# Feed-forward products of a graph layer, in groups of two row blocks instead of four

## The chip, the cores and the metric

The kernel runs on one core of one Trainium2 chip. The metric is the device time of one execution in microseconds (us). Before the change it was 6551.81 us, the median of three runs (6546.44 to 6563.14). One further execution was recorded by the hardware profiler; its span is 7257.0 us, and every duration below that comes from the profile belongs to that execution.

## The reference

Two layers of a graph network over 10,000 nodes of 512 features and 160,000 edges, all in fp32. Cut to what matters:

```python
# layer 0
h   = relu(layernorm(x))
msg = einsum('nd,rdf->nrf', h, rel_W)[src, edge_type]       # 4 relations
agg = segment_sum(msg, dst) / max(deg, 1)
x1  = layer_norm(h + h @ self_W + agg) * ln1_w + ln1_b
f   = gelu(x1 @ W1 + b1) @ W2 + b2                          # 512 -> 1024 -> 512
x   = x + layer_norm(x1 + f)
# layer 1
h   = relu(layernorm(x))
for W_self, W_neigh, b in both:                             # twice
    h = relu(h @ W_self + (segment_sum(h[src], dst) / max(deg, 1)) @ W_neigh + b)
x   = x + h
```

## The kernel before

Nodes are worked in 79 blocks of 128 rows; the last one, block 78, has 16 rows and is worked first. The program has four stages, one behind the other.

**First stage.** For every block the four relation products of `h` are computed and written to `hall_d` in HBM; beside that, the edge list is turned into lists of row numbers.

**The feed-forward stage** is the one that the change edits. For every block it gathers the message rows of the block from `hall_d`, sums them, normalises, does the two feed-forward products, normalises twice more, and writes `h1_d` and `xn_d`. The third and the fourth stage do the same gathers, from `h1_d` and then from `h2_d`, with two products of 512 x 512 per block.

**Gathers.** `gather` (L655 to L671) issues them on GpSimd's queue (POOL), each an indirect DMA of 128 rows of 2 KB: five `orow` tiles (called others), then eleven `row` tiles (called mine), and before them a `tail` tile every fourth and every sixteenth block. That makes 1276 gathers in each of the three gather stages. All but the tails go through one ring of `RING = 28` buffers (L648), which serves the three stages; a gather can be issued when the tile 28 places before it has been read. Others and tails are summed by seven fp32 products with 0/1 matrices on TensorE (`sums`, L688), mine by eleven adds on VectorE into the same PSUM tile (`add`, L700). In the profile an fp32 product is two MATMUL rows, each with its own weight load.

**Slots.** The order is written out by hand (manual schedule): engines run their instructions in program order. The loop over blocks makes one slot per block. In a slot for block b, VectorE first adds the second residual of blocks that were fed forward one slot ago (`second`, L851), then adds the mine rows of b and computes the statistics of b; TensorE does the part of the feed-forward work that stands next in `queue`; ScalarE computes the square roots of the statistics (`now.finish`, L829) and the normalised rows (`scaled`, L837), issued ahead of the last item of that part; the slot ends with the gathers and the sum products of block b+1 (`begin`).

**Groups.** `Group` holds four blocks (128 x 512 moving columns). `turn` (L772, L774) transposes the normalised block on TensorE into one of two PSUM tiles and scales it into `x1T` on ScalarE; it stands in the middle of the slot after the block's own. `up` (L784, L786) makes one of eight 128-column parts of `x1 @ W1` for all four blocks, eight MATMUL rows of 512 columns into one of two PSUM banks, and applies Gelu. `down` (L795) makes a block's product with `W2`, sixteen rows of 512 columns, and issues the load of the residual `xr` on SyncE's queue. `parts` cuts a group into four slots: four `up`, four `up`, two `down`, two `down`. They are queued behind the first slot of the next group.

**The end of the stage.** After the last block, the loop `while queue or fed or third` works off what is queued: half of the ups and all downs of the last group of four, and the ups and downs of a last pair. The row numbers are then shifted by two bits on VectorE (L953), since the later tables have one row per node, and the third stage begins. Its gathers read `h1_d`, so that the first one waits until the last write of `h1_d` (L867) has landed.

Of the kernel before, what the change touches and what calls it, by code (L numbers as in the profile page):

```python
# [16 lines left out]
P = 128  # L17
# [4 lines left out]
def kernel(  # L22
# [621 lines left out]
    def aligned(ctxa):  # L644

        gat = ctxa.enter_context(tc.tile_pool(name="gat", bufs=1))
        psA = ctxa.enter_context(tc.tile_pool(name="psA", bufs=2, space=PSUM))
        RING = 28  # L648
        rest = list(range(full))
        blocks = ([full] if N % P else []) + rest  # L650

# [51 lines left out]
        with ExitStack() as s:  # L703
            wp = s.enter_context(tc.tile_pool(name="wp2", bufs=1))
            gp = s.enter_context(tc.tile_pool(name="gp", bufs=1))
            sp = s.enter_context(tc.tile_pool(name="sp", bufs=3))
            psT = s.enter_context(tc.tile_pool(name="psT2", bufs=2, space=PSUM))
            psH = s.enter_context(tc.tile_pool(name="psH", bufs=2, space=PSUM))
            psO = s.enter_context(tc.tile_pool(name="psO", bufs=2, space=PSUM))
            w1s = wp.tile([P, KC, F], F32, name="w1s")  # L710
            w2s = wp.tile([P, FC, D], F32, name="w2s")
# [5 lines left out]
            def pair(t, b, n, name, bufs):  # L717

                return (gp.tile([P, 2, D], F32, name=name, bufs=bufs)[:height(b), :n],
                        rows_of(t, (b, n, height(b))))  # L720
# [10 lines left out]
            def load_res(b, n):  # L731
                v, at = pair(xr_d, b, n, "xr", 3)
                nc.sync.dma_start(v, at)
                for c in range(n):
                    xrs[b + c] = v[:, c, :]
                xrs[b, n] = v
# [22 lines left out]
            class Group:  # L759


                def __init__(self, bs):
                    self.bs, self.r = bs, height(bs[0])
                    self.xT = gp.tile([P, KC, 4 * P], F32, name="x1T", bufs=2)
                    self.hid = None

                def turn(self, b, v):
# [7 lines left out]
                                             AF.Identity, bias=ln1bc[:, k:k + 1],  # L775
                                             scale=ln1wc[:, k:k + 1])

                def up(self, f):
                    n = len(self.bs) * self.r
                    if self.hid is None:  # L780
                        self.hid = gp.tile([P, FC, 4 * P], F32, name="hid")
                    ph = psH.tile([P, 4 * P], F32, name="ph")
                    for k in range(KC):
                        nc.tensor.matmul(ph[:, :n], w1s[:, k, f * P:(f + 1) * P],  # L784
                                         self.xT[:, k, :n], start=(k == 0), stop=(k == KC - 1))
                    nc.scalar.activation(self.hid[:, f, :n], ph[:, :n], AF.Gelu,  # L786
                                         bias=b1s[:, f:f + 1], scale=1.0)

                def down(self, b):
                    c, r = self.bs.index(b), self.r  # L790
                    if c % 2 == 0:
                        load_res(b, min(2, len(self.bs) - c))
                    po = psO.tile([P, D], F32, name="po")
                    for f in range(FC):
                        nc.tensor.matmul(po[:r], self.hid[:, f, c * r:(c + 1) * r], w2s[:, f, :],  # L795
                                         start=(f == 0), stop=(f == FC - 1))
                    return b, po

                def parts(self):

                    ups = [lambda f=f: self.up(f) for f in range(FC)]
                    downs = [lambda b=b: self.down(b) for b in self.bs]
                    return [ups[:FC // 2], ups[FC // 2:]] + [downs[i:i + 2]
                                                             for i in range(0, len(downs), 2)]

            COLS = 8

# [32 lines left out]
            rests = {}  # L840
            fed, third = [], []
            now = Scales()

            def second():

                nonlocal fed
                got = []
                for b, po in fed:
                    r = height(b)
                    v = rests.pop(b)  # L850
                    nc.vector.tensor_tensor(v[:r], po[:r], v[:r], op=OP.add)  # L851
                    got.append((b, v, now.stats(v[:r], r)))
                fed = []
                return got

            def scaled(got, first):

                nonlocal third, now
                if first:
                    b, c = first  # L860
                    r, v = height(b), nodes[b]
                    now.apply(v[:r], v[:r], c, r, AF.Identity)
                if third:
                    h1, at = pair(h1_d, third[0][0], len(third), "h1", 2)
                    for k, (b, c) in enumerate(third):
                        now.apply(h1[:, k, :], xrs.pop(b), c, height(b), AF.Relu)
                    nc.sync.dma_start(at, h1)  # L867
                third = []
                for b, v, c in got:
                    r = height(b)  # L870
                    now.apply(v[:r], v[:r], c, r, AF.Identity)
                if first:
                    b, c = first
                    r, v = height(b), nodes[b]
                    rests[b] = gp.tile([P, D], F32, name="rest", bufs=11)
                    nc.vector.tensor_tensor(rests[b][:r], v[:r], ln1w[:r], op=OP.mult)
                    nc.vector.tensor_tensor(rests[b][:r], rests[b][:r], lnb2[:r], op=OP.add)
                now = Scales()
                for b, v, c in got:
                    r = height(b)  # L880
                    nc.vector.tensor_tensor(v[:r], v[:r], ln2w[:r], op=OP.mult)
                    nc.vector.tensor_tensor(xrs[b], xrs[b], v[:r], op=OP.add)
                    third.append((b, now.stats(xrs[b], r)))
                if got:
                    b, n = got[0][0], len(got)
                    nc.sync.dma_start(rows_of(xn_d, (b, n, height(b))), xrs.pop((b, n)))

            plan = [[b] for b in blocks[:len(blocks) - len(rest)]]
            plan += [rest[:-2][i:i + 4] for i in range(0, len(rest) - 2, 4)] + [rest[-2:]]
            queue = []  # L890
            turning = None
            held = begin(blocks[0], hots(blocks[0]), table)

            def products(work, turned):


                nonlocal fed
                got = []
                for i, call in enumerate(work):
                    if i == len(work) - 1:  # L900
                        yield
                    if i == len(work) // 2 and turned:
                        turned()
                    got.append(call())
                if not work:
                    yield
                    if turned:
                        turned()
                fed = [g for g in got if g]

            i = 0
            grp = None
            for bs in plan:
                for b in bs:
                    r = height(b)
                    if b == bs[0]:
                        before, grp = grp, Group(bs)
                    if i + 2 < len(blocks):
                        load(blocks[i + 2])
                    if i + 1 < len(blocks):  # L920
                        hot = hots(blocks[i + 1])
                    got = second()
                    pa, mine = held
                    add(b, pa, mine)
                    v = nodes[b]
                    nc.vector.scalar_tensor_tensor(v[:r], pa[:r], rdeg[:r, b:b + 1], v[:r],
                                                   op0=OP.mult, op1=OP.add)
                    first = (b, now.stats(v[:r], r))
                    part = products(queue.pop(0) if queue else [], turning)
                    next(part)  # L930
                    now.finish()
                    scaled(got, first)
                    next(part, None)
                    if i + 1 < len(blocks):
                        held = begin(blocks[i + 1], hot, table)

                    if b == bs[0] and before:
                        queue += before.parts()
                    turning = lambda g=grp, b=b, v=v: g.turn(b, v)
                    i += 1  # L940
            turning()
            queue += grp.parts()
            while queue or fed or third:
                got = second()
                part = products(queue.pop(0) if queue else [], None)
                next(part)
                now.finish()
                scaled(got, None)
                next(part, None)


        for t in (row, orow, *srow):
            nc.vector.tensor_scalar(t, t, R.bit_length() - 1, None, op0=OP.logical_shift_right)  # L953
        quads = [[full]] + [rest[i:i + 4] for i in range(0, full, 4)]
        place = {b: (q, c) for q, bs in enumerate(quads) for c, b in enumerate(bs)}
        for step, (h_d, ws, wn, bs) in enumerate(((h1_d, ws1, wn1, bs1), (h2_d, ws2, wn2, bs2))):
# [388 lines left out]
```

## Time and profile before

| stretch | from, us | to, us | length, us |
|---|---|---|---|
| first stage, to the first gather of rows | 0 | 1514.47 | 1514.47 |
| gathers of the feed-forward stage | 1514.47 | 3417.5 | 1903.03 |
| no gather: the queue is worked off | 3417.5 | 3537.08 | 119.58 |
| gathers of the third stage | 3537.08 | 5359.3 | 1822.22 |
| no gather | 5359.3 | 5394.85 | 35.55 |
| gathers of the fourth stage | 5394.85 | 7225.03 | 1830.18 |
| end | 7225.03 | 7257.0 | 31.97 |

The stretches are read from the start and length of the indirect DMA instructions on POOL in the timeline. Over the whole span TensorE's matmuls (PE) are busy for 78 percent, POOL for 52, VectorE (DVE) for 50 and ScalarE (ACT) for 14. Busy shares do not say which engine bounds a stage; for that one looks at what an engine needs for one block if it never waits, and at what its waits end with. A busy time of PE counts the pipeline of a matmul, so that the spacing of matmuls has to be taken from starts, not from the mean durations.

### The profile page before, as it was taken

The numbers are of one execution on the slowest core, as the hardware profiler recorded it, in microseconds if no ns is written. First come the engines' busy times: TensorE is split into PE (matmuls) and PEld (weight loads), VectorE is DVE, ScalarE is ACT, GpSimd is POOL, SyncE is SP. The second block draws the span as 40 slices with busy tenths as digits, with TensorE's granted clock in tenths as the row PEclk, the third lists the DMA queues.
The fourth block names the chain that finished last, engine by engine and source line by source line (L and its number), as shares of the span: only waits on it lengthen the run. The fifth ranks groups of instructions, "written<-read, shape, count | busy, mean of one in ns | idle before, by whom it ended". The sixth has DMA issues, their size and how long they took to land.

```text
span 7257.0 us, 49943 instructions
## 1 busy us (share of the span) xinstructions
PE 5628.8 (78%) x14251; PEld 2540.8 (35%) x14251; DVE 3650.8 (50%) x7301; ACT 1019.6 (14%) x1667; POOL 3807.2 (52%) x3927
## 2 busy tenths in 40 slices
PE   8999999967888899888676666666666666666666
PEld 4444444423333334333333323332322232333232
DVE  6467786235666666666334333443434444444444
ACT  1000000012222333322210010101000000000000
POOL 0001110046666666665366666666656666666665
PEclk9999999988999999999888888888887888888888
DMA  4223232256777777775466667666666777776775
GB/s 168 93 105 112 95 117 88 84 178 191 215 222 223 224 231 221 213 216 182 154 206 207 204 203 210 205 205 205 205 206 209 218 210 213 221 218 213 218 223 169
DMA packets 457021, 1360.83 MB, mean 188 GB/s; under 512 B 71902, under 2 KB 71902, under 8 KB 446606
## 3 DMA queue, kind: packets, MB, share of 16 engines
q0 software_dynamic: 308768, 1008.91, 47.1%
q1 hardware_dynamic: 136174, 265.65, 10.3%
q10 hardware_dynamic: 11792, 82.97, 2.8%
q8 instruction: 114, 1.87, 0.1%
q14 instruction: 173, 1.42, 0.1%
HBM read 1150.25 MB, written 207.01 MB: 187 GB/s over the span
## 4 chain that ended last, share of the span: by engine, by line
PE 35%; issue 23%; another core or an unknown queue 17%; DVE 4%; ACT 3%; POOL 2%; DMA 1%; ACTq 0%; POOLq 0%; DVEq 0%; SPq 0%
PE pa L688 10%; PE ph L784 6%; PE pm L621 5%; PE po L795 5%; PE po L992 4%; PE po L1026 3%; DVE pa L700 2%; POOL rows L661 2%; PE pT L167 1%; ACT hTb L168 1%; ACT mTb L168 1%; ACT mb L1022 0%; DMA rows<-hall_d,row 0%; DMA rows<-h_d,row 0%
## 5 line engine op out<-in xcount | busy, mean ns | idle before, releaser
L700 DVE TENSOR_TENSOR pa<-pa,rows 128x512 f32<-128x512 f32 x2574 | 1798.5, 699 | 991.1 <-issue 676.5
L661 POOL DMA_INDIRECT rows<-h_d,row x1716 | 1668.4, 972 | 917.5 <-issue 422.8
L661 POOL DMA_INDIRECT rows<-hall_d,row x858 | 854.2, 996 | 516.7 <-issue 193.0
L688 PE MATMUL pa<-rows,hot 128*128 128x512 f32 (+1 forms) x2358 | 1082.1, 606 | 40.0 <-issue 28.0
L992 PE MATMUL po<-wns,mTb 128*128 128x512 f32 (+1 forms) x1264 | 687.2, 694 | 537.8 <-ACT mTb L168 274.5
L1026 PE MATMUL po<-wss,hTb 128*128 128x512 f32 (+1 forms) x1264 | 710.8, 715 | 507.3 <-ACT hTb L168 393.0
L621 PE MATMUL pm<-wrel,hT 128*128 128x512 f32 (+1 forms) x2528 | 1097.8, 592 | 0.0
L661 POOL DMA_INDIRECT rows<-h_d,orow x786 | 754.7, 960 | 404.3 <-issue 223.9
L784 PE MATMUL ph<-x1T,w1s 128*128 128x512 f32 (+2 forms) x1344 | 588.0, 591 | 163.0 <-issue 88.9
L621 PEld LDWEIGHTS pm<-wrel,hT 128*128 128x128 f32 (+1 forms) x2528 | 477.3, 189 | 607.6 <-issue 584.6
L688 PEld LDWEIGHTS pa<-rows,hot 128*128 128x128 f32 (+1 forms) x2358 | 454.3, 193 | 636.5 <-issue 607.8
L661 POOL DMA_INDIRECT rows<-hall_d,orow x393 | 373.2, 950 | 453.3 <-SPq L1341 327.3
L992 PEld LDWEIGHTS po<-wns,mTb 128*128 128x128 f32 (+1 forms) x1264 | 275.6, 224 | 934.5 <-issue 631.3
L795 PE MATMUL po<-w2s,hid 128*128 128x512 f32 (+1 forms) x1264 | 564.2, 598 | 33.5 <-issue 28.7
L1026 PEld LDWEIGHTS po<-wss,hTb 128*128 128x128 f32 (+1 forms) x1264 | 277.4, 231 | 888.6 <-ACT hTb L168 448.9
L688 PE MATMUL pa<-tail,hot 128*128 128x512 f32 x936 | 465.6, 615 | 69.5 <-issue 60.7
L998 DVE TENSOR_TENSOR po<-po,bss 128x512 f32<-128x512 f32 (+1 forms) x79 | 55.0, 696 | 815.9 <-remote 740.7
L494 POOL DMA_INDIRECT win<-rec_d,at x79 | 80.4, 1018 | 661.9 <-issue 568.9
L784 PEld LDWEIGHTS ph<-x1T,w1s 128*128 128x128 f32 x1344 | 258.7, 200 | 461.7 <-issue 375.1
L624 DVE TENSOR_TENSOR ha<-pm,brel 128x512 f32<-128x512 f32 (+1 forms) x316 | 217.0, 687 | 389.5 <-PE pm L621 388.9
L1002 DVE TENSOR_TENSOR ob<-po,bss 128x512 f32<-128x512 f32 (+1 forms) x79 | 54.5, 690 | 608.8 <-remote 283.1
L795 PEld LDWEIGHTS po<-w2s,hid 128*128 128x128 f32 (+1 forms) x1264 | 237.1, 190 | 318.9 <-issue 310.8
(237 smaller groups left out, 4144.6 us busy)
## 6 DMA issues: line engine op xcount, KB each, us to landing
hall_d<-ha ACTq DMA_DIRECT2D x78, 1024.0 KB
hb<-h_d SPq DMA_DIRECT2D x38, 1024.0 KB
rows<-h_d,row POOLq DMA_INDIRECT x1716
xs<-xs_d SPq DMA_DIRECT2D x39, 512.0 KB
xr<-xr_d SPq DMA_DIRECT2D x39, 512.0 KB
xn_d<-xr SPq DMA_DIRECT2D x39, 512.0 KB
h_d<-h SPq DMA_DIRECT2D x39, 512.0 KB
xg<-in_x_dram SPq DMA_DIRECT2D x19, 1024.0 KB
```

Source lines behind the costliest of these rows:

```text
L167: nc.tensor.transpose(p[:, k, :r], rows[:, k * P:(k + 1) * P], ident[:r, :r])
L168: nc.scalar.copy(dest, p[:, :, :r])
L494: nc.gpsimd.indirect_dma_start(out=win[:, c, :], out_offset=None, in_=rec_d, in_offset=bass.IndirectOffsetOnAxis(ap=at[:, c:c + 1], axis=0))
L621: nc.tensor.matmul(pm[:r], hT[:, k, :r], w[:, k, :], start=(k == 0), stop=(k == KC - 1))
L624: nc.vector.tensor_tensor(ha[:r, j - 1, :], pm[:r], brel[:r, (j - 1) * D:j * D], op=OP.add)
L661: nc.gpsimd.indirect_dma_start(out=t[:n], out_offset=None, in_=table, in_offset=bass.IndirectOffsetOnAxis(ap=idx, axis=0))
L688: nc.tensor.matmul(pa[:r], hot[:, t, :r], others[t], start=(t == order[0]), stop=(t == order[-1]))
L700: nc.vector.tensor_tensor(pa[:r], pa[:r], t[:r], op=OP.add)
L784: nc.tensor.matmul(ph[:, :n], w1s[:, k, f * P:(f + 1) * P], self.xT[:, k, :n], start=(k == 0), stop=(k == KC - 1))
L795: nc.tensor.matmul(po[:r], self.hid[:, f, c * r:(c + 1) * r], w2s[:, f, :], start=(f == 0), stop=(f == FC - 1))
L992: nc.tensor.matmul(po[:r], mT[:, k, :r], wns[:, k, :], start=False, stop=(k == KC - 1))
L1026: nc.tensor.matmul(po[:r], hT[:, k, :r], wss[:, k, :], start=(k == 0), stop=False)
```

## The change

- Groups have two blocks instead of four. `x1T` and `hid` have half the width, and `hid` has two buffers instead of one. An `up` makes two of the eight parts (2 x 8 MATMUL rows of 256 columns) into the two halves of one PSUM bank, then applies Gelu to each half. PSUM: three banks for `up` instead of two, one for `turn` instead of two.
- `parts` gives work items with a weight (four `up` of 1, two `down` of 2), and `products(left)` takes items until a weight of `left` is queued. In the slot behind a pair's second block, that block's `turn` now comes first, then both `down` of the pair before; in the next slot all four `up` of the pair, with the next block's `turn` in the middle.
- At the end the queue is worked off in steps that leave 8, 4, 2 and 0. The shift of the row numbers moves into this loop, behind the last `down`.
- `RING` is 32 instead of 28, `rest` has 8 buffers instead of 11.
- `h1`, `xn` and `xr` are written and loaded by pairs, as before.

```diff
-        RING = 28
+        RING = 32
...
-            psT = s.enter_context(tc.tile_pool(name="psT2", bufs=2, space=PSUM))
-            psH = s.enter_context(tc.tile_pool(name="psH", bufs=2, space=PSUM))
+            psT = s.enter_context(tc.tile_pool(name="psT2", bufs=1, space=PSUM))
+            psH = s.enter_context(tc.tile_pool(name="psH", bufs=3, space=PSUM))
...
-                self.xT = gp.tile([P, KC, 4 * P], F32, name="x1T", bufs=2)
+                self.xT = gp.tile([P, KC, 2 * P], F32, name="x1T", bufs=2)
...
-                ph = psH.tile([P, 4 * P], F32, name="ph")
-                for k in range(KC):
-                    nc.tensor.matmul(ph[:, :n], w1s[:, k, f * P:(f + 1) * P],
-                                     self.xT[:, k, :n], start=(k == 0), stop=(k == KC - 1))
-                nc.scalar.activation(self.hid[:, f, :n], ph[:, :n], AF.Gelu,
-                                     bias=b1s[:, f:f + 1], scale=1.0)
+                ph = psH.tile([P, 2, 2 * P], F32, name="ph")
+                for f in (f0, f0 + 1):
+                    for k in range(KC):
+                        nc.tensor.matmul(ph[:, f - f0, :n], w1s[:, k, f * P:(f + 1) * P],
+                                         self.xT[:, k, :n], start=(k == 0),
+                                         stop=(k == KC - 1))
+                for f in (f0, f0 + 1):
+                    nc.scalar.activation(self.hid[:, f, :n], ph[:, f - f0, :n], AF.Gelu,
+                                         bias=b1s[:, f:f + 1], scale=1.0)
...
-                return [ups[:FC // 2], ups[FC // 2:]] + [downs[i:i + 2]
-                                                         for i in range(0, len(downs), 2)]
+                return ([(1, lambda f=f: self.up(f)) for f in range(0, FC, 2)] +
+                        [(2, lambda b=b: self.down(b)) for b in self.bs])
...
+            def products(left, turned=None):
+                work = []
+                while sum(n for n, _ in queue) > left:
+                    work.append(queue.pop(0)[1])
+                if turned:
+                    work.insert(len(work) // 2, turned)
+                for call in work[:-1]:
+                    call()
+                yield
+                for call in work[-1:]:
+                    call()
...
-                    part = products(queue.pop(0) if queue else [], turning)
+                    if whole:
+                        turning()
+                        queue += whole.parts()
+                    part = products(8 if whole else 4, None if whole else turning)
...
+            shares = [8, 4, 2]
             while queue or fed or third:
                 got = second()
-                part = products(queue.pop(0) if queue else [], None)
+                left = shares.pop(0) if shares else 0
+                part = products(left)
                 next(part)
                 now.finish()
                 scaled(got, None)
                 next(part, None)
+                if not left:
+                    shift_rows()
```

## The prediction, made before the changed kernel ran

> **What bounds the kernel now.** I read the 40 slices first, then the busy time by stretch, then the timelines of POOL and PE, last the waits. The slices show that no single engine is full behind the first stage:
>
> ```profile
> PE   8999999967888899888676666666666666666666
> POOL 0001110046666666665366666666656666666665
> DMA  4223232256777777775466667666666777776775
> ```
>
> PE is near its limit in slices 0 to 7 (the first stage, untouched) and again nearly so in the feed-forward stage; POOL stands at six tenths in all three gather stages alike. Cut at the first and the last gather of each stage, the columns being stretch, us, then PE, PEld, DVE, ACT and POOL busy with counts, clock, DMA share and GB/s:
>
> ```profile
> 1514.47:3417.50 1903.03, 1596.05 (x3765) 703.65 (x3766) 1179.23 (x1954) 536.31 (x862) 1252.00 (x1276) 0.90 0.71 218
> 3537.08:5359.30 1822.22, 1225.12 (x2936) 547.88 (x2936) 709.94 (x989) 177.96 (x307) 1227.58 (x1276) 0.83 0.69 206
> 5394.85:7225.03 1830.18, 1204.85 (x2935) 541.32 (x2936) 764.75 (x1070) 135.36 (x232) 1242.82 (x1276) 0.82 0.71 217
> ```
>
> The stages differ widely in PE, DVE and ACT and hardly in length. What they share is 1276 gathers. POOL's timeline shows why: one gather follows another at a fixed step, 0.95 us of work and 0.30 us of gap, whatever the rest does.
>
> ```profile
> 2326.79 0.94 POOL L661 DMA_INDIRECT rows<-hall_d,orow  x1 [0.30 <-issue]
> 2328.04 0.95 POOL L661 DMA_INDIRECT rows<-hall_d,orow  x1 [0.30 <-issue]
> 2329.29 0.95 POOL L661 DMA_INDIRECT rows<-hall_d,orow  x1 [0.30 <-issue]
> ...
> 2346.16 0.95 POOL L661 DMA_INDIRECT rows<-hall_d,row  x1 [5.71 <-PE pa L688]
> ```
>
> The step is 1.253 us, so 1276 take 1599 us; a full block has 16.32 gathers, 20.45 us. The rest of each stretch is almost all long stops like the last line: the steps of 2.3 us and more exceed 1.253 by 262, 226 and 198 us in the three stretches, 686 in all (summed from the starts on POOL). PE, where it isn't stopped, needs 20.18 us for a slot (start of one L784 part to the next):
>
> ```profile
> 2273.92 7.03 PE L784 MATMUL ph<-x1T,w1s 128*128 128x512 f32 x16
> 2280.78 0.60 PE L772 MATMUL pT<-ident,xs 128*128 128x128 f32 x4
> 2281.22 7.03 PE L784 MATMUL ph<-x1T,w1s 128*128 128x512 f32 x16
> 2288.09 1.88 PE L688 MATMUL pa<-tail,hot 128*128 128x512 f32 x4
> 2289.81 4.46 PE L688 MATMUL pa<-rows,hot 128*128 128x512 f32 x10
> 2294.10 7.09 PE L784 MATMUL ph<-x1T,w1s 128*128 128x512 f32 x16
> ```
>
> So in the feed-forward stage POOL (20.45) is just ahead of PE (20.18).
>
> **Profile and timed runs.** The profiled span is 7257.0 us, the timed median 6551.8, 705 less. That is close to the 686 us of long stops: POOL's steps alone give 1514.5 + 3 x 1599 + 119.6 + 35.6 + 32.0 = 6499, 53 below the median. I conclude (it isn't shown) that the timed runs hardly have these stops and run at the gathers' pace. In the profile the waiters of a stop see a finished product late: `x1T` at 2345.46 waited for transposes of 2321.20. So I value the removal of stops at the 53 us left, not at 686.
>
> **What the Trainium skill says.** "TensorE: Matmul & The Clock Gate", section "Back-to-back issue gap", has N / 2.4 + 2.5 ns for a warm matmul of N columns, and says that in a stream of weight loads and matmuls both set the spacing. The trace has two passes per row: 512 columns at (7.03 - 0.59) / 15 = 0.429 us, 256 at (3.62 - 0.41) / 15 = 0.214, exactly half, over weight loads of 0.19 us. The same page, "What's actually happening", has half clock after an idle window of some 3.4 us; the 24 rows in 6.92 us in the fence on the stage's end fit it (after a wait of 3.88). "ScalarE: Activation LUTs", "What ACT_TABLE_LOAD costs", has 1283 ns plus a drain of 1380 ns; the trace has the 1283 and no drain (load at 2310.10, next activation at 2311.39). "PSUM — Partial Sum Buffer", "The four PSUM rules", has banks of 512 fp32, so two halves of 256 fill a bank; no run shows that limit.
>
> **The change, part by part.**
> *Ups of 256 columns.* Per pair 64 rows at 0.214 replace 32 at 0.429: 13.7 us both times. Per slot PE still has 14 + 32 full rows and a turn, 20.18 us. Cost 0; upper bound in the rivals.
> *ACT.* The program has 34 more table loads, 34 x 1.283 = 44 us; 312 Gelus of some 0.43 us (two at 256 columns took 0.86) for 152 of 0.69 add 30 us. ACT is busy 536 of 1903 us, and POOL's 20.45 us per block cover it: 0.
> *Turn at the head of a down slot.* It moves ahead by one down, 16 x 0.429 = 6.9 us. In undisturbed down slots of the trace the normalised rows were ready 8.3 us before the turn (ACT done at 2312.94, turn at 2321.20), so 1.4 us of slack stay. Behind it on PE are both downs and the next sums; VectorE and, through the ring, POOL would wait. Bounds: 0 to some 2.5 us a pair; I take 0, since a wait also hands slack to the next slot.
> *One turn bank, three up banks.* Turns lie at least half a slot apart, and the four copies take 1.4 us: 0. The third bank can only remove waits of `ph` on ACT.
> *DMA queues.* SP issues as many loads and writes as before, at most one slot apart; POOL keeps its order: 0. `rest` lives six slots, eight buffers suffice: 0.
> *Shift of row numbers.* Four DVE operations (0.60 + 0.36 + 0.24 us) already lie beside the wait for `h1_d`: 0.
> *The end of the stage* lies wholly on the path. No gather runs, and the third stage waits for its last write:
>
> ```profile
> 3444.81 0.66 PE L772 MATMUL pT<-ident,xs 128*128 128x128 f32 x4 [1.83 <-ACT xs L837]
> 3445.30 3.60 PE L784 MATMUL ph<-x1T,w1s 128*128 128x512 f32 x8
> 3449.63 10.57 PE L784 MATMUL ph<-x1T,w1s 128*128 128x512 f32 x24 [0.73 <-ACT hid L786]
> 3460.03 27.63 PE L795 MATMUL po<-w2s,hid 128*128 128x512 f32 x64
> 3487.50 3.62 PE L784 MATMUL ph<-x1T,w1s 128*128 128x256 f32 x16
> 3491.29 5.45 PE L784 MATMUL ph<-x1T,w1s 128*128 128x256 f32 x24 [0.18 <-ACT hid L786]
> 3500.62 6.92 PE L784 MATMUL ph<-x1T,w1s 128*128 128x256 f32 x24 [3.88 <-ACT hid L786]
> 3507.38 13.90 PE L795 MATMUL po<-w2s,hid 128*128 128x512 f32 x32
> ```
>
> ```profile
> 3537.08 0.95 POOL L661 DMA_INDIRECT rows<-h_d,orow  x1 [119.58 <-DMA h_d<-h]
> ```
>
> Behind the last turn PE runs from 3445.3 to 3521.3, 76.0 us: four ups, eight half ups, six downs, waits. Afterwards what is left there is two downs, eight half ups, two downs: 32 x 0.429 + 64 x 0.214 + 32 x 0.429 = 41.2 us. The group is smaller, so less is queued, and that work lies in the light first slots instead, where POOL's pace covers it. Saved: 34.8 us (27.4 if the waits stay). The tail from 3521.3 to 3537.1 then handles one block instead of two: one table load (1.28), one block's four DVE operations (2.3) and one activation (0.7) less, 4.3 us. The first gather behind it should wait 119.6 - 39 = 80 us.
> *Ring of 32.* A gather may run four steps, 5.0 us, further ahead. Stops cut by up to 5.0 us each would give 590 us in the profile; in the timed runs at most the 53 us above. I take 0 and keep 53 for the range.
>
> Sum: -34.8 - 4.3 = -39 us: 7257.0 to 7218 in the profile if its stops stay, and 6551.8 - 39 = 6513 timed.
>
> **The rivals.**
> *A, the ring counts.* For it: the three stretches have 162 such stops, and they end when a buffer comes free (on PE, DVE or an unknown releaser); in the third stage PE and DVE have room to catch up. Against: the sum above leaves only 53 us. Time 6513 - 53 = 6460.
> *B, nothing is left:* PE, 0.27 us per block from being the bound, falls behind by about what the end saves (0.5 us in each of 78 slots). Against it: PE ran four slots at 20.2 us without a wait. Time 6551.
> *C, slower: PE waits for the turn* in down slots, 39 times. PE has 2 x 0.27 = 0.54 us of slack a pair; if the rows come 1.4 + 3.0 us later than in that trace, 39 x (3.0 - 0.54) = 96 us come in: 6609. It decides from 1.4 + 0.54 us of lateness, and outweighs the 39 us from 1.0 us more. For it: the chain through adds, statistics, root and activation is in order behind the last mine row. Against: from 1735 us on, no down slot of the trace has less than 8.3 us at the turn's present place. Spacing of 256-column rows above 0.222 us would act alike.
>
> **How the numbers follow.** Likeliest 0.56, range 6500 to 6530; A 0.20; B 0.12; C 0.12. A change of 0.3 percent, 20 us, is about what a measurement here can tell. Faster: most of the likeliest and A, 0.74; same: B and the rest of the likeliest, 0.14; slower 0.12. The range runs from A, with room for a timed step slightly below 1.253 us, to the middle between B and C: 6445 to 6580.
>
> **What would show it.** The wait of the first third-stage gather near 80 us; 41 us of PE work behind the last turn; 256-column rows every 0.214 us; slots of both kinds at 20.2 us where nothing stops; no waits of L772 on ACT. A first-gather wait still near 120, or stops at the head of down slots, would prove me wrong; a third and fourth stage shorter in the timed sum by more than 20 us each would mean the ring.

## The result, and the profile after

After the change the kernel takes 6523.66 us, the median of four runs (6520.63 to 6531.55), against 6553.04 us for four runs of the kernel before (6546.44 to 6563.14). The ratio is 0.9956, its 95 percent interval 0.9938 to 0.9973: 29 us less, where 39 were forecast.

One thing has to be said before any trace is read. The chips on which these runs were made fall into two kinds. On some the kernel before takes about 6555 us, on others 7213 to 7276, every time, and no chip was seen in both kinds. Whether the chip itself makes the difference, or something that ran beside the kernel on it, no run shows; "kind of chip" stands for either. The timed runs of the forecast came from the first kind; the profile before, with its span of 7257.0 us, looks in every stretch like the second kind (run e1 below, 7220.91 us). The profile after has a span of 6518.9 us and is like the first kind. So the two must not be set side by side: the partner of the profile after is e6, the kernel before profiled on a chip where it takes 6555.78 us.

The 40 slices of the kernel after (tenths of busy time) first:

```profile
PE   8999999998999999999887777777778777777777
POOL 0001111005777777777477777777767777777776
DMA  4322222216878888887677777777778777777776
```

POOL stands at seven tenths in all three gather stages. For the kernel after, in us: stretch, length, then PE, PEld, DVE, ACT and POOL busy with counts, clock, DMA share, GB/s:

```profile
1514.10:3166.56 1652.46, 1597.30 (x5088) 916.32 (x5089) 1198.16 (x2001) 623.51 (x1075) 1261.88 (x1276) 0.99 0.81 253
3232.65:4854.23 1621.58, 1258.13 (x2982) 532.99 (x2982) 721.19 (x1009) 176.19 (x312) 1233.23 (x1276) 0.89 0.77 233
4871.88:6498.80 1626.92, 1254.11 (x2982) 531.21 (x2982) 774.34 (x1086) 136.23 (x235) 1238.05 (x1276) 0.89 0.79 244
```

And e6, the kernel before, same columns:

```profile
1515.04:3169.62 1654.58, 1557.68 (x3816) 689.52 (x3817) 1191.43 (x1986) 543.40 (x877) 1264.42 (x1276) 0.98 0.81 251
3270.88:4892.41 1621.53, 1267.09 (x2979) 538.53 (x2980) 720.82 (x1009) 176.22 (x312) 1233.17 (x1276) 0.89 0.77 233
4908.65:6537.94 1629.29, 1251.10 (x2982) 530.10 (x2982) 774.20 (x1086) 136.24 (x235) 1239.51 (x1276) 0.89 0.79 244
```

Subtract POOL's busy time from the length of each stretch: 390.6, 388.4 and 388.9 us after, 390.2, 388.4 and 389.8 before. That is 1275 gaps of 0.305 us in all six rows, whatever PE, DVE and ACT had to do. So POOL hardly ever waits for another engine (the longest gap between two gathers of a stretch is 0.84 us after and 1.73 us in e6), and the pace of the gathers sets all three stages. The change added 1272 MATMUL rows to the first row (5088 against 3816) and its length moved by 2.1 us.

What is left is between the stretches. POOL's timeline of the kernel after, with what ended the wait in brackets:

```profile
3165.61 0.95 POOL L661 DMA_INDIRECT rows<-hall_d,row  x1 [0.30 <-issue]
3232.65 0.94 POOL L661 DMA_INDIRECT rows<-h_d,orow  x1 [66.10 <-DMA h_d<-h]
```

The same of e6:

```profile
3270.88 0.94 POOL L661 DMA_INDIRECT rows<-h_d,orow  x1 [101.26 <-DMA h_d<-h]
```

66.1 against 101.3 us: 35 us less at the end of the feed-forward stage. All other parts of the two spans (start, three stretches, gap before the fourth stage, end) add to 3.8 us of the difference of 39.0 between the two profiles. PE's timeline of that end, after:

```profile
3174.75 0.66 PE L772 MATMUL pT<-ident,xs 128*128 128x128 f32 x4 [3.96 <-ACT xs L839]
3175.24 15.60 PE L799 MATMUL po<-w2s,hid 128*128 128x512 f32 x32
3190.67 13.98 PE L786 MATMUL ph<-x1T,w1s 128*128 128x256 f32 x64
3204.48 13.90 PE L799 MATMUL po<-w2s,hid 128*128 128x512 f32 x32
```

And in e6:

```profile
3176.63 0.66 PE L772 MATMUL pT<-ident,xs 128*128 128x128 f32 x4 [2.35 <-ACT xs L837]
3177.13 15.60 PE L784 MATMUL ph<-x1T,w1s 128*128 128x512 f32 x32
3192.56 27.63 PE L795 MATMUL po<-w2s,hid 128*128 128x512 f32 x64
3220.03 3.62 PE L784 MATMUL ph<-x1T,w1s 128*128 128x256 f32 x16
...
3233.14 8.20 PE L784 MATMUL ph<-x1T,w1s 128*128 128x256 f32 x24 [3.88 <-ACT hid L786]
3241.18 13.90 PE L795 MATMUL po<-w2s,hid 128*128 128x512 f32 x32
```

Behind the last turn PE works from 3175.24 to 3218.38 after, 43.1 us, and from 3177.13 to 3255.08 before, 78.0 us. The difference, 34.8 us, is the first term of the forecast to the decimal. Four ups and two downs are no longer there, since the last group is a pair; they make 27.4 us of it. The other 7.4 us are the waits for ScalarE in the ups of the last pair and the slow rows behind them (21.2 us from the first to the last of 64 rows in e6, 13.8 after). The third bank for `up` is not what removes them: in e4 and e7, which have two, these 64 rows take 13.98 us without a wait as well.

### The profile page after: what moved, and what is told of

Same layout as the page of the kernel before. It is cut to its first block, busy times and chain, and to the rows that moved or that the text cites. A ratio compares the mean times of both kernels' runs of the same rounds, so it can differ in the third digit from the quotient of the medians.

```text
span 6518.9 us, 52690 instructions
## 1 busy us (share of the span) xinstructions
PE 5632.7 (86%) x15467; PEld 2694.5 (41%) x15467; DVE 3638.5 (56%) x7301; ACT 1081.2 (17%) x1853; POOL 3817.8 (59%) x3927
## 4 chain that ended last, share of the span: by engine, by line
DMA 39%; PE 16%; DVE 13%; issue 7%; POOL 5%; ACT 2%; another core or an unknown queue 0%; POOLq 0%; DVEq 0%; ACTq 0%; SPq 0%
DMA rows<-h_d,row 18%; DMA rows<-h_d,orow 13%; DMA rows<-hall_d,row 7%; DVE pa L700 6%; PE pm L621 6%; POOL rows L661 5%; PE pa L688 5%; DVE st L824 2%; PE po L1010 1%; PE po L1044 1%; DMA tail<-h_d,srow 1%; PE ph L786 1%; ACT xs L839 1%; DVE xs L939 1%; PE po L799 1%
## 5 line engine op out<-in xcount | busy, mean ns | idle before, releaser
L700 DVE TENSOR_TENSOR pa<-pa,rows 128x512 f32<-128x512 f32 x2574 | 1799.6, 699 | 1946.1 <-DMA rows<-h_d,row 926.7
L688 PE MATMUL pa<-rows,hot 128*128 128x512 f32 (+1 forms) x2358 | 1382.9, 718 | 674.9 <-DMA rows<-h_d,orow 616.0
L661 POOL DMA_INDIRECT rows<-h_d,orow x786 | 786.3, 1000 | 322.5 <-issue 134.9
L1010 PE MATMUL po<-wns,mTb 128*128 128x512 f32 (+1 forms) x1264 | 573.3, 596 | 1.5 <-ACT mTb L168 1.5
L1044 PE MATMUL po<-wss,hTb 128*128 128x512 f32 (+1 forms) x1264 | 573.5, 597 | 0.0
L786 PE MATMUL ph<-x1T,w1s 128*128 128x256 f32 (+1 forms) x2560 | 558.7, 376 | 0.0
L786 PEld LDWEIGHTS ph<-x1T,w1s 128*128 128x128 f32 x2560 | 478.7, 190 | 79.6 <-issue 16.7
L624 DVE TENSOR_TENSOR ha<-pm,brel 128x512 f32<-128x512 f32 (+1 forms) x316 | 217.2, 687 | 389.5 <-PE pm L621 388.9
L1040 ACT ACTIVATE mb<-pa,rdeg 128x512 f32<-128x512 f32 (+1 forms) x158 | 108.5, 687 | 1822.8 <-DVE pa L700 1813.5
L1010 PEld LDWEIGHTS po<-wns,mTb 128*128 128x128 f32 (+1 forms) x1264 | 240.2, 190 | 308.3 <-issue 306.0
L1044 PEld LDWEIGHTS po<-wss,hTb 128*128 128x128 f32 (+1 forms) x1264 | 229.4, 192 | 232.8 <-issue 232.8
L621 PE MATMUL pm<-wself,hT 128*128 128x512 f32 (+1 forms) x632 | 298.2, 615 | 29.6 <-ACT hT L168 29.6
```

Of the source, the lines that this page charges most:

```text
L621: nc.tensor.matmul(pm[:r], hT[:, k, :r], w[:, k, :], start=(k == 0), stop=(k == KC - 1))
L624: nc.vector.tensor_tensor(ha[:r, j - 1, :], pm[:r], brel[:r, (j - 1) * D:j * D], op=OP.add)
L661: nc.gpsimd.indirect_dma_start(out=t[:n], out_offset=None, in_=table, in_offset=bass.IndirectOffsetOnAxis(ap=idx, axis=0))
L688: nc.tensor.matmul(pa[:r], hot[:, t, :r], others[t], start=(t == order[0]), stop=(t == order[-1]))
L700: nc.vector.tensor_tensor(pa[:r], pa[:r], t[:r], op=OP.add)
L786: nc.tensor.matmul(ph[:, f - f0, :n], w1s[:, k, f * P:(f + 1) * P], self.xT[:, k, :n], start=(k == 0), stop=(k == KC - 1))
```

## The experiments

My theory, E, was that the gain is the end of the stage alone. The rivals were that the ring, the banks or the place of the turn counted, and, once the second kind of chip had turned up, that the smaller groups cost something there (S: they have more products, each of which, I supposed, has to be signalled). Comparisons across chips are made by the ratio to the kernel before on the same chip. This is the table of all twelve; the stretch is that of the feed-forward gathers in the profiled run.

| run | chip | median, us | kernel before there | ratio (95%) | stretch | wait of the first third-stage gather |
|---|---|---|---|---|---|---|
| e1 before | 10 | 7220.91 | 7212.94 | single run | 1872.7 | 126.6 |
| e2 ring of 28 | 10 | 7374.19 | 7212.94 | 1.0229 (1.0209 to 1.0250) | 2077.4 | 89.1 |
| e3 turn in the middle | 10 | 7395.19 | 7212.94 | 1.0246 (1.0231 to 1.0262) | 2081.5 | 108.1 |
| e4 old banks | 10 | 7477.57 | 7212.94 | 1.0354 (1.0339 to 1.0369) | 2149.2 | 113.4 |
| e5 after | 14 | 6526.69 | 6555.78 | 0.9956 (0.9942 to 0.9969) | 1662.9 | 66.6 |
| e6 before | 14 | 6559.68 | 6555.78 | single run | 1654.6 | 101.3 |
| e7 groups alone | 15 | 7455.26 | 7275.90 | 1.0247 (1.0225 to 1.0270) | 2145.8 | 89.3 |
| e8 after | 15 | 7432.77 | 7275.90 | 1.0226 (1.0202 to 1.0251) | 2084.1 | 102.1 |
| e9 last turn later | 15 | 7438.87 | 7275.90 | 1.0233 (1.0210 to 1.0256) | 2076.3 | 97.5 |
| e10 before, ups in halves | 2 | 7359.15 | 7268.37 | 1.0128 (1.0092 to 1.0164) | 2006.5 | 121.8 |
| e11 after, half of each up | 2 | 7301.40 | 7268.37 | 1.0039 (1.0023 to 1.0055) | 1972.2 | 79.7 |
| e12 groups alone, last turn later | 2 | 7458.24 | 7258.25 | 1.0265 (1.0241 to 1.0290) | 2132.8 | 87.4 |

**e1, e2, e3, e4: the kernel before once more, and each of three parts of the change undone in the kernel after.** e1 is the unchanged kernel before.

> The kernel before, unchanged, for a second profile. Theory (the gathers' pace bounds the three gather stages in an undisturbed execution, and the long stops of POOL in the first profile of the kernel before belong to that one recorded execution): span near 6550 us, POOL steps of 1.25 us with next to no stop of 2.3 us or more in the three gather stretches (under 30 us in all), each stretch 1600 to 1660 us, and a wait of the first third-stage gather of 95 to 120 us. Rival (the stops belong to the kernel before, and the ring of 32 removed them): a span of 6550 us or more with stops of over 50 us in each of the third and fourth stage.

```diff
-        RING = 32
+        RING = 28
```

> The changed kernel with RING back at 28. Theory (the ring is not what POOL waits for): within 8 us of the changed kernel, about 6524, and POOL steps as regular as there. Rival A (the four more buffers count): slower than the changed kernel by 15 us or more, up to the time before, with new stops in the third and fourth stage.

```diff
                     if whole:
-                        turning()
                         queue += whole.parts()
-                    part = products(8 if whole else 4, None if whole else turning)
+                    part = products(8 if whole else 4, turning)
```

> The changed kernel with the turn in the middle of the down slot again (down, turn, down). Theory (the turn at the head of a down slot costs nothing, since POOL sets the pace): within 6 us of the changed kernel. Rival C (PE waits for the turn at the head): faster than the changed kernel by 10 us or more, which would be the gain that is missing against my 39 us.

```diff
-            psT = s.enter_context(tc.tile_pool(name="psT2", bufs=1, space=PSUM))
-            psH = s.enter_context(tc.tile_pool(name="psH", bufs=3, space=PSUM))
+            psT = s.enter_context(tc.tile_pool(name="psT2", bufs=2, space=PSUM))
+            psH = s.enter_context(tc.tile_pool(name="psH", bufs=2, space=PSUM))
```

> The changed kernel with two PSUM banks for the turn and two for the ups, as before. Theory (neither is waited for): within 6 us of the changed kernel; the ups in the end of the stage, with two banks, may wait up to 4 us for ACT as they did before. Rival (the third bank carries the gain): slower than the changed kernel by 10 us or more, with waits of L786 on ACT.

These four fell on a chip where the kernel before takes 7212.94 us, so the expectations, written for the first kind of chip, could not be tested as meant. Two things came of them all the same. e1 has long stops of POOL again, 219, 184 and 192 us in the three stretches (counted as in the forecast), as in the profile before: they go with the chip, and the timed runs there have them too. And every version of the pairs was slower here, by 2.3 to 3.5 percent, all of it in the feed-forward stretch, which grew by 205 to 276 us; the third and fourth stages of e2, e3 and e4 (1809.9 to 1822.7 us) are those of e1 (1815.4 and 1821.7).

**e5, e6: both kernels on a chip of the first kind.** No edit.

> The changed kernel, unchanged, beside the kernel before once more, because the two measurements so far come from different chips with very different levels (before 6553 and 7213 us). Theory D (on a chip where POOL is stopped, the change loses, because PE's results are seen late there and the pair groups leave PE and ACT less room than groups of four): on a chip with before near 7213, slower than before by 1 to 2.5 percent, 7290 to 7390, nearly all of it in the feed-forward stage; on a chip with before near 6553, again about 6524. Rival A' (the ring of 32 pays where POOL is stopped): on a chip with before near 7213, faster than before, 7100 or less, with fewer stops in the third and fourth stage.

> The kernel before, for its profile beside the changed kernel's on the same chip. On a chip with before near 6553: no stops of POOL, gather stretches of 1600 to 1660 us, and a wait of the first third-stage gather of 95 to 110 us, against 66 after; if that difference is over 35 us, part of it must come back as a longer feed-forward stretch of the changed kernel, since the timed gain is 29. On a chip with before near 7213: as in its two profiles so far, 650 and 595 us of stops.

This repeated the ratio, 0.9956, and gave the partner trace read above. e5 and the profile after differ from e6 in the stretches by +8.4 and -2.1, +0.6 and +0.1, +3.9 and -2.4 us; in the wait of the first third-stage gather by -34.7 and -35.2. The wait is the only difference that both show. That settles E for this kind of chip as far as the whole change goes: ring, banks and turn together are worth nothing measurable in the stretches where they act. Each of them undone alone was not tried on such a chip, so two that cancel are excluded by no run, only by POOL's gaps, which are the same to about 1 us in every stage.

**e7, e8, e9: the groups alone, the kernel after, and another end, on a chip of the second kind.** e7 takes the three edits of e2, e3 and e4 together; e8 has no edit; e9 puts the turn of the last block between the two downs ahead of it, and loads the last residuals earlier:

```diff
-                    if c == 0:
+                    if c == 0 and b not in xrs:
...
-            turning()
...
-                part = products(left)
+                if left == 4:
+                    load_res(rest[-2], 2)
+                part = products(left, turning if left == 8 else None)
```

> The groups of two, the weighted queue and the steps at the end, but with the ring of 28, two banks each for turn and ups, and the turn in the middle of the down slot. Theory (the shorter end is the whole gain): on a chip with before near 6553, within 8 us of the changed kernel, and a wait of the first third-stage gather of 66 to 70 us. Rival (ring, banks or the place of the turn carry part of it): slower than the changed kernel by 10 us or more. On a chip with before near 7213 its three parts each were 160 to 265 us slower than before; together I expect 200 or more.

> The changed kernel, beside e7 on the same chip. On a chip with before near 6553: 29 us faster than before once more. On a chip with before near 7213, theory D: slower than before by 1 to 2.5 percent, 7290 to 7390; rival A': 7100 or less.

> The changed kernel with the last turn placed between the two downs that stand behind it (PE waits 4 us for the last block at that point, and its next rows run at half clock), and with the last load of xr issued two steps ahead (VectorE waits 2.4 us for it). Theory (what lies between the last gather and the write of h1_d is the path): the wait of the first third-stage gather falls from 66 to 57 to 60 us, the time by the same 6 to 9 us. Rival (another work takes the place): 64 us or more.

The kernel after loses 2.3 percent, 157 us, on this chip, and the groups alone lose as much (2.5 percent, 179 us; I had expected 200 or more). So the loss is that of the groups and of their order, and ring, banks and turn together give back some 22 us of 7455, with runs that overlap. e2, with a ring of 28, has the same ratio as e8 with 32, on another chip: no worth of the ring is seen there either. e4 is an odd case. With two `ph` banks and the turn at the head of the slot, the waits of PE in its feed-forward stretch (us in total, times, longest) begin with

```profile
PE ph L786 <- ACT hid L790: 325.0, 20, 21.7
```

a wait that is not in e8's list. With two banks and the turn in the middle (e7) the ratio is only 1.0247. That fits a third bank that is needed because the turn moved, and not for itself; the two runs were on different chips. e9 took 4.6 us off the wait of the first third-stage gather, 102.1 to 97.5, where I had looked for 6 to 9, while its median is 6 us above e8's with overlapping runs: no gain shown.

Where the time of e8 goes: PE's timeline in a bad spell,

```profile
2331.21 7.07 PE L786 MATMUL ph<-x1T,w1s 128*128 128x256 f32 x32
2338.12 0.38 PE L772 MATMUL pT<-ident,xs 128*128 128x128 f32 x2
2339.60 0.27 PE L772 MATMUL pT<-ident,xs 128*128 128x128 f32 x1 [1.10 <-issue]
2341.74 0.37 PE L772 MATMUL pT<-ident,xs 128*128 128x128 f32 x1 [1.87 <-issue]
2344.53 0.59 PE L786 MATMUL ph<-x1T,w1s 128*128 128x256 f32 x1 [2.42 <-issue]
...
2357.18 7.98 PE L786 MATMUL ph<-x1T,w1s 128*128 128x256 f32 x26 [0.84 <-issue]
```

and POOL's beside it:

```profile
2352.39 0.94 POOL L661 DMA_INDIRECT tail<-hall_d,srow  x1 [0.30 <-issue]
2368.01 0.94 POOL L661 DMA_INDIRECT rows<-hall_d,orow  x1 [14.67 <-PE pa L688]
```

For 17 us PE issues single rows 1.4 to 2.8 us apart and waits for nothing that the trace names ("issue"), while POOL goes on gathering until no buffer is free; then POOL stands for 14.67 us behind a product. The granted clock does not start this: it falls to 0.5 at 2341.20 us, after the first of these pauses, and before the spell 32 rows of 512 columns take 13.90 us (at 2311.47), as on chip 14.

What the other engines see of PE's products shows more. In the third stage and the fourth the kernel before copies each transposed tile into `mTb` on ScalarE (L168). In e6 all 158 copies start within 0.4 us of the end of their transposes and of ScalarE's instruction before, whichever is later. In e1, the same kernel, 73 of the 158 start more than 1 us after it. The worst of them, and the product that reads it:

```profile
6627.36 0.60 PE L167 MATMUL pT<-ident,mb 128*128 128x128 f32 x4
6654.96 0.59 ACT L168 COPY mTb<-pT 128x512 f32<-128x512 f32 x1 [31.80 <-remote]
6655.60 5.95 PE L992 MATMUL po<-wns,mTb 128*128 128x512 f32 x8 [24.20 <-issue]
```

The transposes end at 6627.96 and ScalarE, idle, copies them 27.0 us later. What passes between the other engines is not late in e1: where ScalarE waits for VectorE's sums (L1022 behind L700) it starts within 0.4 us of their end, and where PE waits for ScalarE's copy (L992 behind L168) within 0.1 us. So it is the ends of TensorE's products that are made known late there while gathers run; in the first stage, which gathers no rows, one copy out of 79 is over 1 us late on either kind. The trace's own records are worse there too: of the rows of PE that update a semaphore (a counter by which engines wait for each other) in the feed-forward stretch, e6 has the update of every one (1754), e1 of 1315 out of 1734 and e8 of 1570 out of 1955, so that a wait put down to "issue" may be one whose release was not recorded. Why these chips do so no run shows. Every run here, timed ones too, has a span and a granted clock on record, so that the recording itself is not excluded as a part of the cause.

**e10, e11, e12: is it the number of products?** The pairs bring 8 more products per slot: 32 products of 512 columns per four blocks become 64 of 256. e10 gives the kernel before those 8, with their weight loads, and leaves groups, order and columns unchanged:

```diff
-                    for k in range(KC):
-                        nc.tensor.matmul(ph[:, :n], w1s[:, k, f * P:(f + 1) * P],
-                                         self.xT[:, k, :n], start=(k == 0), stop=(k == KC - 1))
+                    for c0 in range(0, n, 2 * P):
+                        c1 = min(n, c0 + 2 * P)
+                        for k in range(KC):
+                            nc.tensor.matmul(ph[:, c0:c1], w1s[:, k, f * P:(f + 1) * P],
+                                             self.xT[:, k, c0:c1], start=(k == 0),
+                                             stop=(k == KC - 1))
```

e11 takes 8 away from the kernel after, by leaving out half of the contraction of every `up`:

```diff
-                        for k in range(KC):
+                        for k in range(KC // 2):
...
-                                             stop=(k == KC - 1))
+                                             stop=(k == KC // 2 - 1))
```

e12 is e7 with the end of e9.

> The kernel before (groups of four) with each up made in two halves of 256 columns of the same bank: the same columns on PE, twice as many products for the ups, so eight more per slot, as the changed kernel has. Theory S (on a chip where PE's results are seen late, the time of a slot grows with the number of products, each of which signals its end, some 0.33 us for each: the feed-forward stage grew by 211 us in 79 slots for 8 more a slot): on a chip with before near 7213 to 7276, slower than before by 150 to 250 us, all in the feed-forward stage. Rival (the groups of two lose there for their order, the place of the turn, or their Gelus): within 50 us of before there. On a chip with before near 6553: within 8 us of before, since 256-column rows follow each other every 0.214 us.

> The changed kernel with half of each up left out (two of the four parts of the contraction, so that the hidden values are not the reference's): as many products per slot as before, and 6.9 us less PE work in every up slot. Theory (POOL's pace bounds the stage where nothing stops it): on a chip with before near 6553, a feed-forward stretch of 1645 to 1665 us as in the changed kernel, and only the end shorter by 6.9 us, in all 5 to 10 us faster than the changed kernel's 6524 to 6527. Rival (PE bounds the stage): the stretch falls to 1620 or less. On a chip with before near 7213 to 7276, theory S: the stretch falls from some 2084 to 1860 to 1900 us, and the time to 20 to 70 us below before; rival: it stays above 2000.

> Groups of two with the ring of 28, two banks each for turn and ups and the turn in the middle of the down slot (as in e7), and the end of e9 (last turn between two downs, last load of xr two steps ahead). On a chip with before near 6553, theory (gathers set the pace, only the end counts): gather stretches of 1645 to 1665, 1620 to 1635 and 1620 to 1635 us as in the changed kernel, a wait of the first third-stage gather of 56 to 63 us against 66, and a time of 6512 to 6526. Rival (ring, banks or the place of the turn count there): one of the three stretches longer than in the changed kernel by over 15 us. On a chip with before near 7213 to 7276: as e7, 1.5 to 3 percent slower than before, the wait some 5 us shorter than its 89.

The feed-forward stretch of e10:

```profile
1515.25:3521.77 2006.52, 1621.91 (x4918) 940.68 (x4919) 1179.01 (x1954) 535.72 (x862) 1248.70 (x1276) 0.89 0.67 207
```

of e11:

```profile
1515.30:3487.54 1972.24, 1392.63 (x3795) 735.40 (x3796) 1186.10 (x1974) 611.00 (x1061) 1245.30 (x1276) 0.85 0.68 211
```

and, on chips 15 and 10, of e8:

```profile
1512.89:3596.98 2084.09, 1698.27 (x4974) 969.74 (x4974) 1175.84 (x1956) 607.61 (x1047) 1244.39 (x1276) 0.87 0.65 200
```

and e1:

```profile
1516.26:3388.99 1872.73, 1597.03 (x3742) 700.15 (x3743) 1175.39 (x1948) 537.31 (x862) 1257.54 (x1276) 0.91 0.72 222
```

e10 has the MATMUL rows of the pairs (4918 recorded, e8 4974) at the work and the order of the fours. It costs 1.28 percent of the kernel, 91 us timed; S had 150 to 250 us, all in the stretch, and its rival less than 50. Between e1 and e10, on two chips, the stretch grows by 134. So splitting the ups alone makes 1.28 of the 2.26 percent that e8 loses on another chip, with these intervals something between a third and four fifths. What it is about them the runs don't say: the rows that update a semaphore grow by 2.9 per slot in e10 (1964 against 1734 in e1) and by 2.8 in e8, not by the 8 that S had supposed. e11 takes most of the loss away, 1.0226 to 1.0039, but its stretch, 1972 us, is not the 1860 to 1900 that S asked for, its time is 33 us above the kernel before and not 20 to 70 below, and it also takes away 3.5 us of PE's 20 us of work per slot (16 rows of 0.216), so it doesn't single out the number. More products do cost time there, but less than S had forecast, and its reason, a signal for each, isn't shown. What the rest is, the order of the slots or ScalarE's longer list, stays open. The waits of VectorE for ScalarE's roots (`rs`) in the feed-forward stretch are 634.1 us in e8 and 140.0 in e1, which looks like ScalarE; but they are 400.8 us in e10 too, where ScalarE has no more to do than in e1. e12 has a wait of 87.4 against e7's 89.3 us; the later turn and the earlier load together are worth 2 to 5 us of that wait, again under what the times can tell.

No version beats both kernels on both kinds of chip. On the second kind the kernel before is the fastest of all; on the first kind only the two kernels ran, and the kernel after is the faster.

## Why the prediction was right, point by point

**What bounds the kernel.** Right where the timed runs were made: the gathers' step of 1.25 us sets the three stages. My reason for saying so was wrong. I took the 705 us between the profiled span and the timed median for something that the profiled execution had and the timed ones lack. By all that the traces show it is a difference of chips: e1's profile (7219.1) and the timed runs of its chip (7212.94) agree. The sum of the stops was wrong too. The 226 us of the third stage included the gap of 35.5 us between two stages; the stops proper are 261.5, 191.0 and 197.8, 650 us in 161 stops, and 705 - 650 leaves 55 us for shorter gaps between the stages and more even steps. The 53 us that I kept as the most a ring could give were not stops either. In e6 the three stretches exceed 3 x 1599 by 108 us, nearly all of it in single gathers that take a little longer than 0.95 us, and its waits between the stages and its end are 50 us shorter than the profile before had them.

**Ups of 256 columns, turn, banks, ScalarE, DMA queues: 0.** Borne out together on the first kind of chip by the equal stretches. PE's timeline after, two slots in the steady state:

```profile
2121.64 0.60 PE L772 MATMUL pT<-ident,xs 128*128 128x128 f32 x4
2122.08 13.90 PE L799 MATMUL po<-w2s,hid 128*128 128x512 f32 x32
...
2141.48 1.13 PE L688 MATMUL pa<-rows,hot 128*128 128x512 f32 x2 [0.32 <-DMA rows<-hall_d,orow]
2142.44 7.07 PE L786 MATMUL ph<-x1T,w1s 128*128 128x256 f32 x32
2149.35 0.60 PE L772 MATMUL pT<-ident,xs 128*128 128x128 f32 x4
```

32 rows of 256 columns take (7.07 - 0.38) / 31 = 0.216 us each, 0.214 forecast. (A row of 512 columns takes 0.429 us, about twice what the formula that the forecast quotes gives; the forecast rightly went by the measured spacing.) The turn at the head of the down slot has no wait. From turn to first up the slot is 20.80 us, and what PE waits for in it is a gathered row that has only just landed: the sign that the gathers lead. Rival C needed waits of L772 on ACT; outside the last turn (3.96 us, e6 2.35) there are none. Rival B needed a longer stretch; it is 1652.5 against 1654.6. Rival A needed shorter third and fourth stages; they are equal.

**The end of the stage.** PE's work behind the last turn: 78.0 to 43.1, -34.8 us, as forecast. The forecast's own two values, 76.0 and 41.2, were each 2 us lower, so the exact match has some luck in it: in both traces PE runs slowly for a while after the wait ahead of the last turn (granted clock 0.5 for 3.41 us; 15.60 us for 32 rows of 512 columns, against 13.90 elsewhere). The tail was mis-sized: from the end of PE's last product to the first gather it is 15.8 us in e6 and 14.3 after, 1.5 us less and not 4.3. DVE's timeline after shows where the other 2.8 went:

```profile
3217.95 0.69 DVE L899 TENSOR_TENSOR xr<-xr,rest 128x512 f32<-128x512 f32 x1 [2.41 <-DMA xr<-xr_d]
3218.68 0.69 DVE L824 BATCH_NORM_STATS2 st<-xr 128x6 f32<-128x512 f32 x1
...
3219.50 0.57 DVE L852 TENSOR_SCALAR row<-row 128x858 int32<-128x858 int32 x1
3219.99 0.36 DVE L852 TENSOR_SCALAR orow<-orow 128x395 int32<-128x395 int32 x1
3220.27 0.24 DVE L852 TENSOR_SCALAR srow<-srow 128x20 int32<-128x20 int32 x2
3220.42 0.68 DVE L865 TENSOR_TENSOR rest<-po,rest 128x512 f32<-128x512 f32 x1
```

The last product ends at 3218.38, and DVE first reads it (L865) at 3220.42. It is late by 2.0 us, since the block before it waited 2.41 us for its residual `xr`, which landed only then, and since the shift of the row numbers stands ahead of L865. I had put the shift at nothing, beside the wait for `h1_d`; it lies on the path for 0.9 us. The late residual is the cause: in e9, which loads it earlier, DVE reads the last product 0.03 us after its end, with the shift still ahead of it, and the tail is 12.3 us against 14.6 in e8. So the forecast's 4.3 us overlooked the load of `xr`; with it in time some 3.5 us (15.8 - 12.3, an estimate across two chips) would have been saved. The turn itself came 1.2 us later behind the last gather. So the end is -34.8 - 1.5 + 1.2 = -35.1 us.

**The numbers.** The wait was to fall to 80 us and is 66.1: the change in it is right within 4 us, the starting value of 119.6 belonged to the other kind of chip (101.3 on this one). The timed gain of 29 us has an interval of 18 to 41 us, which holds both 35 and 39; the stretches of two profiles of the same kernel (after and e5) differ by 17 us in all, so no more can be said of the difference.

**What the prediction did not have.** A slower outcome exists, at 2.3 percent, on chips of the second kind, and it is none of my rivals as I had argued them. For the chip of the profile that I read, the forecast fails: its other value, 7218 us in the profile if the stops stay, stands against profiled spans of 7429.4 us (e8). The step that failed there is the 0 for ups of 256 columns. I had costed PE's time alone, and not that the stops grow with 8 more products per slot: 219 us in the feed-forward stretch of e1, 371 in e10, 442 in e8, on three chips. e10 puts the term at 91 us of the timed run; the rest of the 157 us has no step that a run points to.

## What to carry to other kernels

Set the span of a profile against the times of the same chip before reading it; a gap of ten percent can mean that the trace shows another regime, in which the sign of a change differs. Where three stages with different work have the same length less the busy time of one engine, that engine sets the pace, and an edit of the others pays only where that engine stands idle: count what is queued behind the last turn of a stage, since a smaller group shortens just that. Splitting a product into more and narrower ones at the same PE time is not free everywhere: here it cost 1.3 percent by itself on one kind of chip, and nothing that could be measured, as part of the change, on the other.

## What was not expected of the hardware

The same kernel took 6555.78 us on one chip and 7212.94, 7268.37 and 7275.90 on three others, run after run, with the first stage equal to 2 us (1514.5 to 1516.3 us in the kernel before) and 604 of the 661 us between e1 and e6 in the three stretches with gathers. On the slower chips ScalarE and VectorE saw the ends of TensorE's products up to 27.0 us late while gathers ran, though what passed between the other engines was not late, and TensorE itself paused between rows with no wait in the trace.
